# Preparing layer 1's row tiles during layer 0, and a start in another order

## The chip, the cores and the metric

The kernel runs on one core of a Trainium2 chip. The core has five engines that each work through a queue of their own, in order: TensorE for matmuls (PE in the profile, with its weight loads as PEld), VectorE (DVE), ScalarE (ACT), GpSimd (POOL) and SyncE (SP), which here only issues transfers. Transfers are carried out by 16 DMA engines that the queues share. The metric is the time of one execution on the device in microseconds (us); the time of a kernel is the median of several runs.

## The reference

The kernel computes two layers over 4096 rows of width 512. Each layer normalizes x, takes the positive part h, and adds a term to x.

Layer 0 is attention within 32 graphs of 128 consecutive rows, with a dense 4096 x 4096 matrix `adj` (mostly zeros) as a bias; outside a row's own graph the score is `-1e6` times twice the entry, and its softmax share is then masked to zero, yet counts in the denominator:

```python
h = jnp.maximum(_layernorm(x, axis=-1), 0.0)
query = h @ Wq.T + bq;  key = h @ Wk.T + bk;  value = h @ Wv.T + bv
a = jnp.where(mask, query @ key.T * scale, 0.0)
scores = (a + adj + adj) * jnp.where(mask, 1.0, -1000000.0)
x = x + (jax.nn.softmax(scores, axis=-1) * mask) @ value
```

Layer 1 is graph attention with 8 heads of 64 columns: each row averages the projected rows of its neighbours (`adj > 0`), weighted by `exp(t_j)` (the part of the logit that belongs to the row itself cancels in the softmax):

```python
h = jnp.maximum(_layernorm(x, axis=-1), 0.0)
mx = jnp.einsum('nf,hfd->hnd', h, W)
t_j = jnp.einsum('hnd,hd->hn', mx, a_dst)
attn = jax.nn.softmax(jnp.where(adj[None] > 0, s_i[:, :, None] + t_j[:, None, :], neg_inf), axis=-1)
x = x + concat_heads(jnp.einsum('hij,hjd->hid', attn, mx))
```

## The kernel before

Rows are worked on in 32 tiles of 128. The kernel has a start, layer 0, the rest of layer 1's preparation, and an aggregation.

**Start** (`fold`, line 163). The two weight matrices come in transposed. `fold` loads them, transposes them back on PE in blocks (line 185), and copies the blocks out of PSUM with ScalarE (line 186). It multiplies them into one matrix `m_sb` (line 221, four column blocks of four matmuls), so that a score needs one projection (`gT`, the "queries") and not two. Between the first transposes it spreads the two biases over all partitions by small matmuls against the identity (`spread_bias`, line 168), and VectorE multiplies these rows with the weights to get the bias columns `u_col` and `c_sb` (line 199). In the middle of the `m_sb` matmuls, PE spreads `u_col` into `u_sb` (line 211) and `zp` into `z_sb`.

**Layer 0** goes over 16 pairs of tiles (`for g in range(NG)`, line 525), pipelined: iteration g finishes pair g and starts pair g+1. Its pieces are
- `scores` (466): score matmuls, VectorE adds the diagonal block of `adj`, ScalarE takes the exponential;
- `queries` (408) of the next pair: 16 matmuls, each block copied out by ScalarE as `gT`;
- `turned` (485): the exponentials transposed by PE and copied to `sT` by ScalarE (487);
- for each of the two tiles: `read` (427) of a tile of the next pair, which takes two halves of 1 MB of `adj` that were loaded before, makes byte masks of them (VectorE, 136), sums the exponentials of all entries outside the graph (ScalarE, written to `junk`, 443), copies the diagonal block (GpSimd) and stores the masks to memory as `a_d`; `attend` (493), which multiplies `sT` with the values, adds x and stores the row tile to `x1_d`; `values` (420) of the next pair;
- `normed` (383) of pair g+2: statistics, normalization `hn`, transposes on PE (127), and the column sum `hu` (396).

Up to seven halves of `adj` are in flight (`AB = 7`): a new load is issued on SP when the oldest half has been read. Pairs of x rows (`xg`) have three buffers; SP issues them in the same queue as the halves. PSUM has four tiles named `pp` for queries, values, attention and projections together, and three named `pt` for transposes.

**Preparation of a layer-1 tile.** `normed1` (359) loads a row tile back from `x1_d` on SP, normalizes it and transposes it (127); `prepare` (367) projects it with `w1x` (`project1`, 243: eight matmuls into two `pp` tiles), ScalarE takes the exponential of `t_j`, VectorE multiplies the heads by it (`weigh`, 252), and ScalarE and GpSimd split the result into two parts of lower precision (`split`, 230 and 231). `w1x` is loaded in iteration 2. In the last iteration of layer 0, `prepare_on` is called four times: four row tiles are normalized and three of them are prepared. The loop at line 569 prepares the rest, 29 tiles.

**Aggregation** (line 590): for each of 32 row tiles, `aggregate` reads the masks back, turns them, and runs 96 matmuls over all prepared parts (283). VectorE and PSUM work for the first row tiles, and a check that the graphs are tiles (`graphs_are_tiles`, 298), already runs while the last tiles of layer 1 are prepared.

What sets the order: the program above gives dependences and buffers; a scheduler in the framework then fixes, when the kernel is built, an order of instructions for each engine by its own estimates of their durations. An engine follows that order strictly, and waits where an operand is not there yet. So an instruction can stand in another place of its queue than its line suggests, and a small edit moves others.

Of the kernel before, what the change touches and what calls it, by code (L numbers as in the profile page):

```python
# [51 lines left out]
def kernel(  # L52
# [110 lines left out]
    def fold(sb, tmp, work, ps_t, ps_p):  # L163
# [4 lines left out]
        def spread_bias(b):  # L168
            pp = ps_p.tile([P, D], F32, name="pp")
            for k in range(KC):  # L170
                nc.tensor.matmul(
                    pp[:, ts(k, P)], b[:, k : k + 1].to_broadcast([P, P]), ident,
                    start=True, stop=True,
                )
            row = work.tile([P, D], F32, name="b_row", tag="hn")
            nc.scalar.copy(row, pp)
            return row

        nat = []
        for n, wT in enumerate((wkT_sb, wqT_sb)):  # L180
            w = tmp.tile([P, KC, D], F32, name=f"w{n}", tag="lo")
            for k in range(KC):
                pt = ps_t.tile([P, KC, P], F32, name="pt")
                for m in range(KC):
                    nc.tensor.transpose(pt[:, m, :], wT[:, k, ts(m, P)], ident)
                nc.scalar.copy(w[:, :, ts(k, P)], pt)
                if n == 0 and k == 0:
                    rows = [spread_bias(b) for b in (bk_sb, bq_sb)]
# [6 lines left out]
        z_sb = sb.tile([P, 1], F32, name="z_sb")  # L195
        for dst, wT, row in ((u_col, wqT_sb, rows[0]), (c_sb, wkT_sb, rows[1])):
# [10 lines left out]
        for m in range(KC):  # L207
            if m == 2:
                pp = ps_p.tile([P, D], F32, name="pp")
                for k in range(KC):  # L210
                    nc.tensor.matmul(
                        pp[:, ts(k, P)], u_col[:, k : k + 1].to_broadcast([P, P]), ident,
                        start=True, stop=True,
                    )
                nc.scalar.copy(u_sb, pp)
                pp = ps_p.tile([P, D], F32, name="pp")
                nc.tensor.matmul(pp[:, :1], zp.to_broadcast([P, P]), one, start=True, stop=True)
                nc.scalar.copy(z_sb, pp[:, :1])
            pp = ps_p.tile([P, D], F32, name="pp")
            for k in range(KC):  # L220
                nc.tensor.matmul(
                    pp, wq[:, k, ts(m, P)], wk[:, k, :], start=(k == 0), stop=(k == KC - 1)
                )
            nc.scalar.mul(m_sb[:, m, :], pp, SCALE)
# [116 lines left out]
    with ExitStack() as straight:  # L341
# [4 lines left out]
        with ExitStack() as prep:  # L346
# [30 lines left out]
            with (  # L377
# [5 lines left out]
                def normed(g):  # L383
# [4 lines left out]
                    hns = []  # L388
# [520 lines left out]
```

## Time and profile before

| | us |
|---|---|
| median of 5 runs (lowest to highest) | 977.47 (976.46 to 978.88) |
| the profiled execution's own time | 976.75 |
| its span in the profile | 974.9 |
| PE busy / VectorE / ScalarE / GpSimd | 939.5 / 457.7 / 261.8 / 187.6 |
| first queries of layer 0 on PE | 37.57 |
| last scores of layer 0 on PE | 332.94 |
| aggregation on PE, from | 472.69 |
| aggregation matmuls on PE, busy | 489.6 |

Times in views of the trace count from the start of the span. A matmul on 32-bit operands leaves two records in the trace, so `x32` there is 16 matmuls. Where an engine was idle before an instruction, the trace names what ended the idle time. ScalarE and GpSimd are often idle, which costs nothing by itself; TensorE is idle for about 35 us of the span.

### The profile page before, as it was taken

How to read it: one execution, taken by the hardware profiler on the slowest of the kernel's cores; microseconds unless marked ns; L12 is line 12 of the kernel's file. 1: busy time of each engine (PE TensorE's matmuls, PEld its weight loads, DVE VectorE, ACT ScalarE, POOL GpSimd, SP SyncE). 2: the span in 40 equal slices, each digit the busy share in tenths (PEclk: the TensorE clock that was granted, in tenths of full speed). 3: DMA queues.
4: the chain of work that ended last, by engine and by line, in shares of the span. 5: the costliest groups of instructions: out<-in, count | busy, mean ns of one | idle time of the engine just before them, and what ended most of it. 6: DMA issues, size and time to landing. Idle time of an engine off the chain costs nothing.

```text
span 974.9 us, 13181 instructions
## 1 busy us (share of the span) xinstructions
PE 939.5 (96%) x5051; PEld 816.9 (84%) x5051; DVE 457.7 (47%) x978; ACT 261.8 (27%) x505; POOL 187.6 (19%) x344
## 2 busy tenths in 40 slices
PE   8999999999899979999999999999999999999994
PEld 5676676667666767888899999999999999999994
DVE  4677776667674387555142342423324233242321
ACT  5766666676651223333100000000000000000000
POOL 2221113112211065555110101101011010110100
PEclk9999999999999999999999999999999999999997
DMA  9988989999881232221022313123121221212201
GB/s 342 419 345 337 376 321 363 370 347 350 348 341 54 83 101 87 67 72 58 1 53 79 88 44 87 50 81 85 46 87 49 82 81 50 87 49 82 65 22 37
DMA packets 58042, 148.28 MB, mean 152 GB/s; under 512 B 6386, under 2 KB 23026, under 8 KB 49778
## 3 DMA queue, kind: packets, MB, share of 16 engines
q1 hardware_dynamic: 48178, 130.31, 38.0%
q10 hardware_dynamic: 9792, 17.05, 4.7%
q8 instruction: 41, 0.67, 0.3%
q14 instruction: 31, 0.25, 0.1%
HBM read 113.77 MB, written 33.55 MB: 151 GB/s over the span
## 4 chain that ended last, share of the span: by engine, by line
PE 79%; DMA 10%; DVE 4%; ACT 2%; POOL 1%; issue 1%; SPq 0%; ACTq 0%; DVEq 0%
PE pg L283 50%; PE pp L420 8%; DMA a<-adj 8%; PE pp L243 8%; PE pp L408 7%; PE pp L493 3%; PE pss L466 2%; PE pt L127 1%; ACT junk L443 1%; DMA bv_sb<-bv 1%; DVE row L121 1%; POOL part L231 1%; DVE a L136 1%; POOL rstd L120 1%; DVE stats L114 1%
## 5 line engine op out<-in xcount | busy, mean ns | idle before, releaser
L283 PE MATMUL pg<-part,at 128*128 128x348 f32 x3072 | 489.6, 321 | 1.2 <-DVE e L252 1.2
L283 PEld LDWEIGHTS pg<-part,at 128*128 128x128 f32 x3072 | 489.4, 188 | 1.5 <-issue 1.5
L277 DVE CAST at<-at 128x4096 fp32r<-128x4096 fp8e4 x32 | 73.6, 2300 | 312.2 <-PE pg L283 312.2
L290 ACT COPY tot<-pg 128x522 f32<-128x522 f32 x32 | 19.2, 599 | 470.5 <-PE pg L283 470.5
L443 ACT ACTIVATE junk<-a 128x2048 bf16<-128x2048 f32 (+15 forms) x92 | 124.5, 1353 | 47.6 <-DVE x L495 22.4
L243 PE MATMUL pp<-w1x,hT 128*128 128x256 f32 (+1 forms) x512 | 117.3, 383 | 0.0
L420 PE MATMUL pp<-wv,hT 128*128 128x512 f32 x256 | 114.9, 592 | 0.0
L408 PE MATMUL pp<-hT,m_sb 128*128 128x256 f32 x512 | 113.2, 379 | 0.0
L408 PEld LDWEIGHTS pp<-hT,m_sb 128*128 128x128 f32 x512 | 96.1, 190 | 12.9 <-issue 0.5
L243 PEld LDWEIGHTS pp<-w1x,hT 128*128 128x128 f32 x512 | 94.9, 190 | 13.8 <-issue 0.5
L420 PEld LDWEIGHTS pp<-wv,hT 128*128 128x128 f32 x256 | 48.6, 190 | 60.7 <-issue 60.7
L136 DVE TENSOR_SCALAR a<-a 128x512 fp8e4<-128x512 f32 x256 | 94.5, 450 | 2.0 <-DMA a_d<-a 2.0
L595 POOL COPY den_all<-tot 128x1 f32<-128x1 f32 x31 | 5.8, 186 | 369.1 <-DVE tot L291 369.1
L128 ACT ACTIVATE hT<-pt 128x512 f32<-128x512 f32 x64 | 37.3, 598 | 71.0 <-PE pt L127 71.0
L604 POOL TENSOR_TENSOR tot<-tot,row 128x512 f32<-128x512 f32 x31 | 40.0, 1290 | 61.7 <-DVE tot L296 61.7
L118 POOL TENSOR_SCALAR ve<-mv 128x1 f32<-128x1 f32 x64 | 17.2, 270 | 164.2 <-DVE mv L116 162.7
L231 POOL TENSOR_TENSOR part<-e,part 128x522 fp32r<-128x522 f32 x32 | 42.0, 1311 | 30.8 <-ACT part L230 27.2
L493 PE MATMUL pp<-v,sT 128*128 128x512 f32 x64 | 34.4, 618 | 8.5 <-ACT sT L487 8.0
L424 DVE TENSOR_TENSOR v<-pp,bv_sb 128x512 f32<-128x512 f32 x32 | 22.1, 690 | 42.0 <-PE pp L420 42.0
L270 DVE STREAM_TRANSPOSE at<-mw 128x1024 f32<-128x1024 f32 x32 | 39.6, 1236 | 0.0
L120 POOL TENSOR_TENSOR rstd<-ve,neghalf 128x1 f32<-128x1 f32 x64 | 38.5, 602 | 5.0
L252 DVE TENSOR_TENSOR e<-pp,e 128x256 f32<-128x256 f32 x64 | 26.5, 415 | 23.7 <-ACT e L371 21.0
(93 smaller groups left out, 586.3 us busy)
## 6 DMA issues: line engine op xcount, KB each, us to landing
a<-adj SPq DMA_DIRECT2D x64, 1024.0 KB, 12.5
a_d<-a SPq DMA_DIRECT2D x32, 512.0 KB, 10.8
row<-x_d SPq DMA_DIRECT2D x64, 256.0 KB, 3.2
mw<-a_d SPq DMA_DIRECT2D x128, 128.0 KB, 3.8
xg<-x SPq DMA_DIRECT2D x16, 512.0 KB, 4.5
x_d<-x ACTq DMA_DIRECT2D x32, 256.0 KB, 4.2
out<-tot ACTq DMA_DIRECT2D x31, 256.0 KB, 3.7
wkT_sb<-wkT SPq DMA_DIRECT2D x4, 256.0 KB, 4.9
```

Of the source, the lines that this page charges most:

```text
L120: nc.gpsimd.tensor_tensor(rstd, ve, neghalf, ALU.pow)
L136: nc.vector.tensor_scalar(a8v[:, u], av[:, u], 0.0, None, ALU.is_gt, saturate=False)
L231: nc.gpsimd.tensor_sub(dst[:, :, 1, :], e3, dst[:, :, 0, :].bitcast(F32))
L243: nc.tensor.matmul(pm[g][:, :n], hT[:, k, :], w1x[:, k, g * HW : g * HW + n], start=(k == 0), stop=(k == KC - 1),)
L270: nc.vector.transpose(at8.rearrange("p c n b -> p (c n b)").bitcast(F32).rearrange("p (c u n) -> p c u n", c=NW, n=B), mw.rearrange("p u ( ...
L277: nc.vector.tensor_copy(at.rearrange("p (c b) q -> p c b q", b=BY), at8.rearrange("p c q b -> p c b q"))
L283: nc.tensor.matmul(pg[:, c, : 2 * CW1], at[:, j, :], part(j)[:, c].rearrange("p s w -> p (s w)"), start=(j == 0), stop=(j == NT - 1),)
L408: nc.tensor.matmul(pp[:, : G * P], m_sb[:, k, ts(m, P)], hT[:, k, :], start=(k == 0), stop=(k == KC - 1),)
L420: nc.tensor.matmul(pp, hT[:, k, ts(t, P)], wv[:, k, :], start=(k == 0), stop=(k == KC - 1))
L443: nc.scalar.activation(junk[:, c0:c1], a[:, c0:c1], AF.Exp, scale=2.0 * NEG, accum_out=sums[:, n : n + 1],)
L493: nc.tensor.matmul(po, sT[:, t, :], v, start=True, stop=True)
L604: nc.gpsimd.tensor_add(num, num, row)
```

## The change

Two things change.

In `fold`, ScalarE and VectorE take turns in copying the transposed weights out of PSUM. The bias rows are spread only after all of `m_sb` has been multiplied, and `u_col` and `z` after the bias columns, in place of between the transposes and in the middle of the `m_sb` matmuls.

In layer 0, one layer-1 row tile is taken on in every second iteration from 3 on (3, 5, 7, 9, 11, 13), after `turned` and before the attention matmuls; each such step normalizes one tile and prepares the one before it. The last iteration has three such steps in place of four. So when layer 0 ends, nine tiles are normalized and eight prepared, in place of four and three; the loop after layer 0 prepares 24. `w1x` is loaded in iteration 1 in place of 2. In `normed`, the column sum `hu` of a tile comes right after its transposes. What is computed stays the same.

```diff
@@ fold
-        def spread_bias(b):
...
-                nc.scalar.copy(w[:, :, ts(k, P)], pt)
-                if n == 0 and k == 0:
-                    rows = [spread_bias(b) for b in (bk_sb, bq_sb)]
+                dst = w[:, :, ts(k, P)]
+                if k % 2:
+                    nc.vector.tensor_copy(dst, pt)
+                else:
+                    nc.scalar.copy(dst, pt)
...
+        for m in range(KC):
+            pp = ps_p.tile([P, D], F32, name="pp")
+            for k in range(KC):
+                nc.tensor.matmul(
+                    pp, wq[:, k, ts(m, P)], wk[:, k, :], start=(k == 0), stop=(k == KC - 1)
+                )
+            nc.scalar.mul(m_sb[:, m, :], pp, SCALE)
+        rows = []
+        for n, b in enumerate((bk_sb, bq_sb)):
+            pp = ps_p.tile([P, D], F32, name="pp")
+            for k in range(KC):
+                nc.tensor.matmul(
+                    pp[:, ts(k, P)], b[:, k : k + 1].to_broadcast([P, P]), ident,
+                    start=True, stop=True,
+                )
+            row = work.tile([P, D], F32, name=f"b_row{n}", tag="hn")
+            nc.scalar.copy(row, pp)
+            rows.append(row)
         for dst, wT, row in ((u_col, wqT_sb, rows[0]), (c_sb, wkT_sb, rows[1])):
...
-        for m in range(KC):
-            if m == 2:
-                pp = ps_p.tile([P, D], F32, name="pp")
-                for k in range(KC):
-                    nc.tensor.matmul(
-                        pp[:, ts(k, P)], u_col[:, k : k + 1].to_broadcast([P, P]), ident,
-                        start=True, stop=True,
-                    )
-                nc.scalar.copy(u_sb, pp)
...
-            nc.scalar.mul(m_sb[:, m, :], pp, SCALE)
+        pp = ps_p.tile([P, D], F32, name="pp")
+        for k in range(KC):
+            nc.tensor.matmul(
+                pp[:, ts(k, P)], u_col[:, k : k + 1].to_broadcast([P, P]), ident,
+                start=True, stop=True,
+            )
+        nc.scalar.copy(u_sb, pp)
+        pp = ps_p.tile([P, D], F32, name="pp")
+        nc.tensor.matmul(pp[:, :1], zp.to_broadcast([P, P]), one, start=True, stop=True)
+        nc.scalar.copy(z_sb, pp[:, :1])
@@ normed
-                    hns = []
                     for t in range(G):
                         hn = sb.tile([P, D], F32, name="hn")
                         norm(xg[g][:, t, :], hn)
                         relu_T(ps_t, hn, hT[:, :, ts(t, P)])
-                        hns.append(hn)
-                    for t, hn in enumerate(hns):
                         hu = sb.tile([P, D], BF16, name="hu", bufs=1)
@@ the loop of layer 0
-                    if g == 2:
+                    if g == 1:
                         w1x = load_w1(pool1, sb)
...
-                    def prepare_on():
-                        if last:
+                    def prepare_on(now):
+                        if now:
                             i = len(ahead)
                             ahead.append(normed1(i))
                             if i:
                                 prepare(i - 1, ahead[i - 1], part_tile(lo, i - 1))
 
                     s = scores(g, hT, gT, r, *look)
-                    prepare_on()
-                    prepare_on()
+                    prepare_on(last)
                     if not last:
                         ngT = queries(nhT)
                     sT = turned(s)
+                    prepare_on(3 <= g and g % 2)
                     nvs = []
                     for t in range(G):
                         look_on(t)
                         attend(sT, vs[t], g, t)
-                        prepare_on()
+                        prepare_on(last and t == 0)
                         if not last:
                             nvs.append(values(nhT, t))
```

## The prediction

> **What bounds the kernel now.** I read the page's shares first, then the chain that ended last in order of time, then the timeline of TensorE (PE) in three stretches: the start, layer 0, and the passage from layer 0 to layer 1.
>
> ```profile
> PE 939.5 (96%) x5051; PEld 816.9 (84%) x5051; DVE 457.7 (47%) x978; ACT 261.8 (27%) x505; POOL 187.6 (19%) x344
> ...
> PE   8999999999899979999999999999999999999994
> ...
> DMA  9988989999881232221022313123121221212201
> ...
> PE 79%; DMA 10%; DVE 4%; ACT 2%; POOL 1%; issue 1%; SPq 0%; ACTq 0%; DVEq 0%
> ```
>
> PE is busy in nearly every slice, in layer 0 too, where the DMA engines are also about 90% busy. So a change that only moves PE work can win no more than PE's idle time. Where that lies, PE's timeline shows. (Columns: start, length, instruction; in brackets the idle time before it and what ended it. One matmul leaves two records.) The start:
>
> ```profile
> 9.95 2.33 PE L185 MATMUL pt<-ident,wqT_sb 128*128 128x128 f32 x16
> 12.12 7.03 PE L221 MATMUL pp<-w,w 128*128 128x512 f32 x16
> 18.99 1.05 PE L211 MATMUL pp<-ident,u_col 128*128 128x128 f32 x8
> 19.88 0.28 PE L217 MATMUL pp<-one,zp 128*128 128x1 f32 x2
> 20.51 7.13 PE L221 MATMUL pp<-w,w 128*128 128x512 f32 x16 [0.35 <-ACT m_sb L224]
> 27.48 1.04 PE L127 MATMUL pt<-ident,hn 128*128 128x128 f32 x8
> 30.52 0.33 PE L127 MATMUL pt<-ident,hn 128*128 128x128 f32 x1 [2.00 <-DVE hn L121]
> 30.69 7.04 PE L420 MATMUL pp<-wv,hT 128*128 128x512 f32 x16
> 37.57 7.07 PE L408 MATMUL pp<-hT,m_sb 128*128 128x256 f32 x32
> ```
>
> From the bias sums to the first queries at 37.57 PE rests only 2.4 us: while it multiplies the weights, VectorE (DVE) finishes the bias columns and the first normalization. Layer 0:
>
> ```profile
> 54.92 1.13 PE L493 MATMUL pp<-v,sT 128*128 128x512 f32 x2 [0.61 <-ACT sT L487]
> ...
> 170.26 1.13 PE L493 MATMUL pp<-v,sT 128*128 128x512 f32 x2 [1.57 <-ACT sT L487]
> ...
> 189.31 1.12 PE L493 MATMUL pp<-v,sT 128*128 128x512 f32 x2 [0.74 <-ACT sT L487]
> ...
> 208.99 1.13 PE L493 MATMUL pp<-v,sT 128*128 128x512 f32 x2 [0.71 <-ACT sT L487]
> ...
> 249.23 1.13 PE L493 MATMUL pp<-v,sT 128*128 128x512 f32 x2 [2.90 <-ACT sT L487]
> ```
>
> With 0.61 at 111.57, 0.27 at 131.35 and 0.61 at 287.18, PE idles 8.0 us in 16 iterations, each time for sT. ScalarE (ACT) copies sT in its queue behind Exp pieces that wait for adjacency halves: in the chain the half asked for at 235.11 takes 11.35 us, and Exp, gT and sT follow before PE goes on at 249.23. The passage to layer 1:
>
> ```profile
> 351.52 0.66 PE L127 MATMUL pt<-ident,row 128*128 128x128 f32 x4 [2.23 <-DVE row L121]
> ...
> 365.36 0.66 PE L127 MATMUL pt<-ident,row 128*128 128x128 f32 x4 [3.28 <-DVE row L121]
> ...
> 388.93 0.60 PE L127 MATMUL pt<-ident,row 128*128 128x128 f32 x4
> 389.37 3.67 PE L243 MATMUL pp<-w1x,hT 128*128 128x264 f32 x16
> ```
>
> With 0.54, 0.78 and 0.50 more, 7.3 us of idle before the steady rhythm of 3.95 us a tile (transposes 0.44, projection 3.51).
>
> **Part by part. 1, the start.** I follow the built order of the changed kernel through its in-order queues with the durations above.
> - Alternate weight copies go to DVE, but between the first and second DVE copy the order has the statistics of the first x pair, whose load ends DVE's wait at 12.90 before. Two statistics (1.29), then the copy (no DVE row; ACT's takes 0.61, DVE's bias add from PSUM 0.69; I take 0.6): 14.8. Wq's last transposes (0.6) and a further DVE copy need it, so the weight products start near 15.7, not 12.12.
> - All sixteen now run in one piece, two groups of 6.9: to 29.6. The bias sums follow, 0.89 each (from 18.99 to 19.88): to 30.5 and 31.4. Before, they lay between the first transposes.
> - The bk row's copy (0.59) ends at 31.2. Only then can DVE make u_col. Its queue holds four column sums of u_col and one of c_sb (0.73 apart), two mask pieces (0.35) and then the first hn (0.54): 36.1.
> - PE transposes (0.45). ACT is in Exp pieces of 0.6, 1.8 and 2.1 with u_sb between, until about 37.5, so hT is there at 38.1 and PE does one values matmul. The next PE work is the transposes of tile 1's hn, which DVE reaches after three column sums, three masks and hu (4.4): 40.5. Transposed at 41.0; three matmuls of tile 0 (2.6) and four of tile 1 (3.4) end at 47.0.
>
> Queries thus start 47.0 - 37.57 = 9.4 us later; behind them wait every score and attention matmul, so it is on the path: +9.5. Ends: had the products started at 12.12 and nothing else moved, +6; +12 if PE runs cold. For that, the bk sums at 4.74 cost 1.9 us per 8 records, the same shape warm 1.05. Against it, after a gap of 3.28 us transposes took 0.66, after none 0.60, and my gaps are at most 1.8 us; no cold surcharge is taken. [...]
>
> **2, five projections and six row transposes inside layer 0.** Moved work is five times 3.51 and six times 0.44, 20.2 us of PE, out of the loop after layer 0 and into iterations 3 to 13; the last iteration keeps three projections. PE pays it in either place, and there the cover is only the 8.0 us of idle. Per moved tile the other queues get: SP one 256 KB row load (landing 3.2); DVE statistics, aggregate and norm (0.69, 0.17, 0.55) and two weighings (0.41 each); POOL two small steps (0.3, 0.6), the split (1.24) and a copy (0.19); ACT hT, Exp and cast (0.60, 0.18, 0.63). DVE, ACT and POOL are busy 33, 33 and 11 of 50 us in layer 0, so they fit; six row loads are 1.6 MB beside some 100 MB.
> - The projection lies between turned and attend in iterations 5, 7, 9, 11, 13, so sT has 3.5 us more there: the 0.74 of iteration 7 goes. The larger waits (1.57, 0.71, 2.90) fall in even iterations 6, 8, 10, which have no projection. They gain only by the extra 3.95 us that loads get in every second iteration; the three equal waits of 0.61 look like the floor, so at most 3.4 goes. SP does not use all of that time: its order puts the next x pair (which waits for both attends) ahead of adjacency loads, and it issued nothing from 238.4 to 255.46. I take -3.0 in all. Ends: -8.0 (all goes), and a loss, in the rivals.
> - Row loads sit on SP between adjacency loads, about one iteration ahead of the DVE statistics that wait for them; behind those wait masks and the values' bias add. A late row would cost up to 4.5 us, x's median landing time; issued 15 us ahead, nothing.
> - A split is 1.24 us alone and was 3.22 at 346.83 beside DVE's CAST; a diag copy 0.28 alone, 2.36 amid masks at 23.07. So five splits may take 3 us each in layer 0. POOL has 39 of 50 us free: nothing on the path. [...]
>
> **3, the passage.** PE waits there for row norms, and DVE carries two adjacency transposes and casts (1.24, 2.3 each) and the graph checks (sixteen steps of 0.42) among them. All of that stays, next to as many tiles. In the new order PE has one projection more ahead of the fifth row, but the sixth row now stands behind the second transpose and cast, which held the seventh before. I take -0.5; ends -7.3 and +3.
>
> **4, small edits.** w1x loads one iteration earlier (1.25 MB, landing 7.1, before adjacency loads on SP) and its eight DVE steps (0.68) move with it: 0, ends -1 and +1, since iterations 1 and 2 had no PE wait. hu right after each hn moves 0.68 us on DVE under 18 us iterations: 0. Aggregation, 489.6 us on PE, is untouched.
>
> **Sum.** +9.5 - 3.0 - 0.5 = +6.0 on the profiled execution's 976.75, thus 982.75. That execution was 0.72 below the median of 977.47, so for the median 983.5.
>
> **Rivals.** No change that can be told is within 0.2% (2.0 us), 975.5 to 979.4.
> - *Faster: the prepared tiles fill PE's waits.* Place: sT waits of layer 0 and norm waits of the passage. If the lead of prepared tiles removed all but 2.5 of 15.3 us, the sum is 9.5 - 12.8 = -3.3: 974. It decides once more than 9.5 + 2 is filled. For it: every wait has other PE work ready in principle. Against: PE runs in order, and the large waits are in iterations without a projection.
> - *Same: the late start is absorbed.* Loads run from the first microseconds whatever PE does, so a PE that starts 9.5 us later finds its adjacency there and the 8.0 go: +1.0, 978.5. Against: only seven halves fit, and the first wait of over 0.7 us came at 170, long after such a lead is spent.
> - *Much slower: a new wait on PSUM.* A projection takes two of four PSUM tiles that the second attend and values need 4.3 us later; the weighings that free them stand behind eight to fourteen masks (0.35 each, 2.8 to 4.9) and take 0.8, and masks wait for loads. It decides where masks and weighings outlast 4.3 us after the projection; at 2.5 us in five iterations, +12.5 on top: 995. For it: 3.6 to 5.7 stands against 4.3. Against: DVE idles a third of the time, so most of these masks can be done before the projection is.
>
> **How the numbers follow.** My forecast 0.58 (its own range 979.5 to 988), faster 0.13, same 0.13, much slower 0.16. Near the lower edge of the forecast a little falls to same. So faster 0.14, same 0.14, slower 0.72; the range 974 to 992 leaves out about half of the outer two.
>
> **What would show it.** Right: queries (line 406 then) start at 45 to 49, with idle before values; sT waits of at most 0.7 at most iterations; passage gaps of 5 to 8 us; aggregation starting 5 to 8 us later than 472.69. Wrong: queries before 43, waits of over 2 us before second attends, or passage gaps under 3 us.

## The result, and the profile after

The changed kernel takes 981.6 us (median of 50 runs, 977.48 to 984.8), the kernel before 978.5 us (median of 92 runs beside it). The ratio is 1.0030, with a 95% interval from 1.0022 to 1.0038: 2.9 us slower, where 6.0 us were forecast. The profiled execution took 980.02 us, with a span of 978.1, against 976.75 and 974.9 before: +3.2 us in the span.

The granted clock of PE differs too. Its mean is 0.992 over 68 recorded executions of the kernel before and 0.989 over 52 of the changed one, and within the kernel before the longer executions tend to be those with the lower clock (975.81 us at 0.995, 986.23 us at 0.986). By an estimate from these means, 0.003 of 978 us is 2.9 us of full clock more that was not granted; how much of it fell on work that the end waits for, these records do not tell.

The page of the changed kernel, in the same rows (busy time of each engine; busy tenths of PE in 40 slices; the clock granted to PE; the DMA engines; shares of the chain that ended last):

```profile
PE 943.3 (96%) x5051; PEld 817.6 (84%) x5051; DVE 461.2 (47%) x982; ACT 259.6 (27%) x501; POOL 187.1 (19%) x344
...
PE   6899999999999998899999999999999999999995
...
PEclk9899999999999999999999999999999999999998
DMA  9949999899983123322012222122231222312201
...
PE 86%; DMA 4%; DVE 3%; ACT 2%; POOL 2%; issue 1%; SPq 0%; ACTq 0%; DVEq 0%; POOLq 0%
```

PE is still the bound, and has as many instructions as before. What differs is at the left: the first slice of PE has 6 tenths in place of 8, and the second a granted clock of 8 tenths in place of 9. The third slice of the DMA row, 4 in place of 8, says that early in layer 0 the loads rest for a while: SP issued no adjacency load between 49.05 and 72.69 us. Before those loads its queue holds the load of a pair of x rows, which was issued at 71.03, as the second attention result of the first iteration was ready; in the kernel before that load went out at 61.27.

The windows view sums this up by stretch: from the start to the first queries, to the last scores of layer 0, to the first aggregation matmul, to the end. Its columns are the window, its length, then busy time and instructions of PE, PEld, DVE, ACT and POOL, the granted clock of PE, the DMA share and GB/s. After:

```profile
0.00:47.33 47.33, 35.73 (x114) 19.60 (x115) 26.96 (x74) 25.47 (x39) 7.53 (x27) 0.89 0.98 384
47.33:358.84 311.51, 307.76 (x1312) 215.40 (x1311) 205.19 (x545) 179.56 (x346) 71.47 (x129) 0.99 0.75 289
358.84:476.74 117.90, 110.54 (x555) 93.86 (x553) 75.19 (x167) 34.89 (x84) 61.10 (x125) 1.00 0.24 70
476.74:978.10 501.36, 489.27 (x3073) 488.79 (x3073) 153.86 (x196) 19.73 (x33) 46.96 (x63) 0.99 0.22 63
```

Before, these four stretches had lengths of 37.57, 295.37, 139.75 and 502.21 us. With the 20.2 us of moved PE work put back in its old place, the differences are:

| stretch | forecast | measured (profile) |
|---|---|---|
| start | +9.5 | 47.33 - 37.57 = +9.76 |
| layer 0 | -3.0 | 311.51 - 20.2 - 295.37 = -4.06 |
| passage | -0.5 | 117.90 + 20.2 - 139.75 = -1.65 |
| aggregation to the end | 0 | 501.36 - 502.21 = -0.85 |
| sum | +6.0 | +3.2 |

The start of the changed kernel on PE:

```profile
13.73 0.76 PE L174 MATMUL pt<-ident,wqT_sb 128*128 128x128 f32 x4 [3.21 <-DVE w L177]
14.29 15.53 PE L190 MATMUL pp<-w,w 128*128 128x512 f32 x32
...
36.11 1.09 PE L127 MATMUL pt<-ident,hn 128*128 128x128 f32 x4 [0.70 <-DVE hn L121]
38.47 2.08 PE L418 MATMUL pp<-wv,hT 128*128 128x512 f32 x2 [1.27 <-ACT hT L128]
40.34 1.06 PE L127 MATMUL pt<-ident,hn 128*128 128x128 f32 x4
41.19 6.30 PE L418 MATMUL pp<-wv,hT 128*128 128x512 f32 x14
47.33 1.03 PE L406 MATMUL pp<-hT,m_sb 128*128 128x256 f32 x4
```

The chain is the one foreseen: PE waits 3.21 us for a weight copy that stands behind the statistics of x on VectorE, then come the products, the late bias sums, and the first normalized tiles in two pieces. Two lengths are new. The products take 15.4 us, from 14.29 to the bias sums at 29.65, where before two halves of 6.9 us were enough; and the sixteen values records take 2.08 + 6.30 = 8.38 us, where before they took 7.04.

The waits for `sT` in layer 0, 8.0 us before, are now three, 3.3 us in all; around the first of them PE did this (the matmuls that the turned scores feed are in line 491 here, values in 418):

```profile
82.73 1.04 PE L127 MATMUL pt<-ident,hn 128*128 128x128 f32 x8
85.71 2.00 PE L491 MATMUL pp<-v,sT 128*128 128x512 f32 x2 [1.95 <-ACT sT L485]
87.51 4.46 PE L418 MATMUL pp<-wv,hT 128*128 128x512 f32 x8
91.81 1.02 PE L491 MATMUL pp<-v,sT 128*128 128x512 f32 x2
92.66 3.60 PE L418 MATMUL pp<-wv,hT 128*128 128x512 f32 x8
96.10 1.95 PE L464 MATMUL pss<-hT,gT 128*128 128x128 f32 x16
```

The same pair of instructions for the two tiles takes 91.81 - 85.71 = 6.10 us, and then 96.10 - 91.81 = 4.29. So the wait of 1.95 us cost 1.8 more in slow matmuls behind it. That is the clock, and it explains the long records of the start as well. Granted clock in small windows (the columns are window, length, PE busy, clock, DMA share, GB/s):

```profile
14.00:14.50 0.50, 0.50 (x5) 0.64 1.02 426
14.50:15.00 0.50, 0.50 (x1) 0.50 1.06 442
...
17.50:18.00 0.50, 0.50 (x2) 0.95 0.83 344
...
34.50:35.00 0.50, 0.39 (x2) 0.62 0.94 385
...
41.00:41.50 0.50, 0.50 (x3) 0.55 0.91 369
41.50:42.00 0.50, 0.50 (x2) 1.00 1.05 434
85.50:86.00 0.50, 0.29 (x1) 0.82 0.93 393
...
89.00:89.50 0.50, 0.50 (x2) 0.77 1.06 442
```

Next to the mixed windows the record reads 1.00 on one side and 0.50 on the other (1.00 from 14.00 to 14.10, 0.50 from 14.20 to 14.30), so a mean of 0.64 is read as 0.28 of the window at full clock and the rest at half. Read so, the clock is halved from 14.14 to 17.55, from 34.62 to 41.45, and from 85.82 to 89.23: for 3.4, 6.8 and 3.4 us.

In the passage the waits for normalized rows are 0.38, 3.02, 1.20 and 1.54 us, 6.1 in place of 7.3; the longest and the last of them:

```profile
388.00 0.66 PE L127 MATMUL pt<-ident,row 128*128 128x128 f32 x4 [3.02 <-DVE row L121]
...
404.76 0.66 PE L127 MATMUL pt<-ident,row 128*128 128x128 f32 x4 [1.54 <-DVE row L121]
```

### The profile page after: what moved, and what is told of

Same layout as the page of the kernel before. It is cut to its first block, busy times and chain, and to the rows that moved or that the text cites. A ratio compares the mean times of both kernels' runs of the same rounds, so it can differ in the third digit from the quotient of the medians.

```text
span 978.1 us, 13164 instructions
## 1 busy us (share of the span) xinstructions
PE 943.3 (96%) x5051; PEld 817.6 (84%) x5051; DVE 461.2 (47%) x982; ACT 259.6 (27%) x501; POOL 187.1 (19%) x344
## 4 chain that ended last, share of the span: by engine, by line
PE 86%; DMA 4%; DVE 3%; ACT 2%; POOL 2%; issue 1%; SPq 0%; ACTq 0%; DVEq 0%; POOLq 0%
PE pg L284 50%; PE pp L418 10%; PE pp L406 9%; PE pp L244 8%; DMA a<-adj 3%; PE pp L491 3%; PE pss L464 2%; PE pt L127 2%; PE pp L190 2%; ACT junk L441 1%; POOL part L232 1%; DMA xg<-x 1%; DVE a L136 0%; DVE row L121 0%; ACT gT L410 0%
## 5 line engine op out<-in xcount | busy, mean ns | idle before, releaser
L418 PE MATMUL pp<-wv,hT 128*128 128x512 f32 x256 | 117.1, 600 | 1.3 <-ACT hT L128 1.3
```

What stands on the lines that cost most here:

```text
L418: nc.tensor.matmul(pp, hT[:, k, ts(t, P)], wv[:, k, :], start=(k == 0), stop=(k == KC - 1))
```

## The experiments

My theory after the result: the change is two independent things, a start that loses time and moved preparations that gain less. The rival: the late start by itself takes waits out of layer 0, so that the parts don't add. Twelve kernels tell about this. In the table, "idle" is the stretch from the first queries to the last scores less PE's busy time in it, and "sT" is the part of the idle that ended with the copy of turned scores; both are of one profiled execution. The ratio is to the kernel before, run beside it on the same chip.

| kernel | median us | ratio (95%) | queries from | idle | sT | aggregation from |
|---|---|---|---|---|---|---|
| before | 978.5 | 1 | 37.57 | 8.5 | 8.0 | 472.69 |
| changed | 981.6 | 1.0030 (1.0022 to 1.0038) | 47.33 | 3.8 | 3.3 | 476.74 |
| moves + small edits | 972.2 | 0.9941 (0.9921 to 0.9961) | 39.07 | 5.2 | 2.4 | 469.83 |
| start alone | 984.9 | 1.0070 (1.0047 to 1.0094) | 48.26 | 4.4 | 3.8 | 478.81 |
| moves, even iterations | 972.5 | 0.9934 (0.9910 to 0.9958) | 39.03 | 4.6 | 2.2 | 469.44 |
| small edits alone | 978.4 | 1.0000 (0.9982 to 1.0018) | 37.31 | 8.5 | 8.1 | 474.95 |
| changed, copies by ScalarE | 976.4 | 0.9985 (0.9967 to 1.0003) | 45.65 | 3.7 | 3.4 | 474.39 |
| changed, bias sums early | 976.8 | 0.9992 (0.9976 to 1.0007) | 41.86 | 5.8 | 2.6 | 476.84 |
| before + 10.4 us of PE | 985.2 | 1.0073 (1.0045 to 1.0100) | 47.27 | 6.7 | 6.1 | 481.82 |
| changed + fillers | 979.0 | 1.0015 (0.9995 to 1.0034) | 48.17 | 3.2 | 2.8 | 475.42 |
| before + 3.5 us of PE | 978.2 | 0.9990 (0.9967 to 1.0014) | 39.79 | 8.4 | 8.0 | 474.11 |
| before + 20.8 us of PE | 999.0 | 1.0184 (1.0149 to 1.0220) | 54.87 | 11.4 | 11.0 | 494.08 |
| moves + small edits + 3.5 us | 973.5 | 0.9937 (0.9910 to 0.9963) | 40.12 | 2.7 | 2.4 | 467.56 |
| moves alone | 969.2 | 0.9886 (0.9853 to 0.9919) | 37.35 | 2.8 | 2.3 | 466.02 |

**Moves and small edits, with the old start.** `fold` is that of the kernel before.

```diff
@@ fold, against the changed kernel
...
-                dst = w[:, :, ts(k, P)]
-                if k % 2:
-                    nc.vector.tensor_copy(dst, pt)
-                else:
-                    nc.scalar.copy(dst, pt)
+                nc.scalar.copy(w[:, :, ts(k, P)], pt)
+                if n == 0 and k == 0:
+                    rows = [spread_bias(b) for b in (bk_sb, bq_sb)]
...
```

> The kernel before with the new layer 0 (preparation in iterations 3 to 13, w1x loaded in iteration 1, hu after each hn) and the old start. Theory A, two independent parts: the queries start near 37.6 again, the shorter idle of layer 0 and of the passage stays, 5 to 7 us faster than before, ratio 0.993 to 0.995. Rival B, the late start is what let the adjacency loads get ahead and so emptied the waits of layer 0: most of the gain goes, at most 2 us faster, ratio 0.998 to 1.001, with sT waits of 6 us or more in layer 0.

Measured: 0.9941, that is 5.8 us under the kernel before. Of sT waits, 8.0 us before, 2.4 are left. One new wait came, for a row that VectorE had not normalized in time:

```profile
218.56 0.44 PE L127 MATMUL pt<-ident,row 128*128 128x128 f32 x2 [2.46 <-DVE row L121]
```

So the moves are worth more than the 3.5 us forecast for layer 0 and the passage together.

**The new start alone.** The loops are those of the kernel before.

```diff
@@ the loop of layer 0, against the changed kernel
...
-                    if g == 1:
+                    if g == 2:
                         w1x = load_w1(pool1, sb)
...
-                    prepare_on(3 <= g and g % 2)
...
```

> The kernel before with the new start alone. Theory A: queries start near 47.3, and nothing gives the 9.8 us back: ratio 1.008 to 1.011. Rival B: PE starts later but finds its adjacency halves ready, layer 0's 8.0 us of waits shrink to 3 or 4: ratio 1.004 to 1.006, with last scores only 5 to 6 us later than 332.94.

Measured: 1.0070, +6.8 us, between the two expectations, for a start that is 10.7 us late. The rest did not come from preparations, for none was moved. The profile shows where it went: layer 0 has four sT waits in place of eight.

```profile
159.96 1.13 PE L494 MATMUL pp<-v,sT 128*128 128x512 f32 x2 [0.27 <-ACT sT L488]
198.72 1.13 PE L494 MATMUL pp<-v,sT 128*128 128x512 f32 x2 [1.43 <-ACT sT L488]
237.73 1.12 PE L494 MATMUL pp<-v,sT 128*128 128x512 f32 x2 [1.67 <-ACT sT L488]
275.46 1.13 PE L494 MATMUL pp<-v,sT 128*128 128x512 f32 x2 [0.40 <-ACT sT L488]
```

The waits, 3.8 us in sum, are those that the rival expected. The late start is partly absorbed, then. The forecast's argument against it (seven buffers are soon used up) did not hold.

**The preparations in even iterations.** The prediction gave a reason by parity: sT is covered only in iterations that hold a projection.

```diff
@@ the loop of layer 0, against moves + small edits
-                    prepare_on(3 <= g and g % 2)
+                    prepare_on(4 <= g and g % 2 == 0)
```

> As the first of these runs, but with the preparation in iterations 4, 6, 8, 10, 12 and 14, where the kernel before had its larger waits for sT (1.57, 0.71, 2.90 in iterations 6, 8, 10). If the projection helps by lying between turned and attend, this variant hides these waits directly: 1 to 2 us faster than the odd one. If it helps by giving the loads more time in every second iteration, the two are within 1 us of each other.

Measured: 0.9934 against 0.9941, and the sT waits 2.2 against 2.4 us. So the time does not depend on which iterations hold the projections, and the waits of iterations 6, 8 and 10 are gone with either choice: a projection beside the wait is not needed to take it away. A wait for a row of 1.97 us came here too, at 236.63.

**The small edits alone** (the earlier `w1x`, and `hu` after each `hn`).

```diff
@@ against the kernel before
-                        hns.append(hn)
-                    for t, hn in enumerate(hns):
...
-                    if g == 2:
+                    if g == 1:
                         w1x = load_w1(pool1, sb)
```

> The kernel before with only the two small edits: w1x loaded in iteration 1, hu right after each hn. Theory A: no difference that can be told, ratio 0.999 to 1.001. Rival C, the small edits reorder the queues of layer 0 and are themselves a part of its gain: ratio 0.995 to 0.998.

Measured: 1.0000, with the same sT waits in sum as before (8.1 us). They are worth nothing alone, as forecast. One more thing is in this profile: the wait at iteration 10, the longest of the kernel before, here has slow matmuls behind it, which it had not there.

```profile
249.16 2.07 PE L490 MATMUL pp<-v,sT 128*128 128x512 f32 x2 [2.92 <-ACT sT L484]
...
260.89 1.95 PE L463 MATMUL pss<-hT,gT 128*128 128x128 f32 x16
```

Before, that matmul took 1.13 us after a wait of 2.90, and the next scores came 257.91 - 249.23 = 8.68 us after its start, not 260.89 - 249.16 = 11.73. The granted clock from 250 to 254 is 0.50 here and was 1.00 there. The same wait can cost its own length, or that and a stretch at half clock, which cost 3.1 us here.

**All weight copies by ScalarE.**

```diff
@@ fold, against the changed kernel
                 dst = w[:, :, ts(k, P)]
-                if k % 2:
-                    nc.vector.tensor_copy(dst, pt)
-                else:
-                    nc.scalar.copy(dst, pt)
+                nc.scalar.copy(dst, pt)
```

> The changed kernel, but ScalarE alone copies the transposed weights, so that no weight copy stands behind the statistics of x on VectorE. In the changed kernel the last four transposes waited 3.21 us for such a copy, the products began at 14.29 instead of 12.12 and took 15.4 us instead of 13.9, at a granted clock of 0.77 to 0.81 in their first slices. Theory A (the copy costs both its wait and a cold clock behind it): the products begin at 11.5 to 12.2 and take 13.9, the queries begin at 43 to 44 instead of 47.33. Rival (no clock surcharge from the wait): the products begin there, take 15.4 still, and the queries begin at about 45. For the whole: if the start were simply added to the rest, the time falls by 3.5 to 4 us against the changed kernel, to 977.5 to 978; if the waits of layer 0 share in it (they shrink when the start is later), by 1.5 to 2.5, to 979 to 980. The order built for ScalarE and TensorE in layer 0 is that of the changed kernel.

Measured: 0.9985, that is 1.0030 - 0.9985 = 0.45% or 4.4 us under the changed kernel.

```profile
12.99 14.22 PE L187 MATMUL pp<-w,w 128*128 128x512 f32 x32
...
33.51 0.63 PE L127 MATMUL pt<-ident,hn 128*128 128x128 f32 x4 [1.01 <-DVE hn L121]
35.57 2.08 PE L415 MATMUL pp<-wv,hT 128*128 128x512 f32 x2 [1.43 <-ACT hT L128]
37.44 1.11 PE L127 MATMUL pt<-ident,hn 128*128 128x128 f32 x4
38.34 7.48 PE L415 MATMUL pp<-wv,hT 128*128 128x512 f32 x14
```

The wait for the copy is gone and the products take 14.1 us again: the bias sums begin at 27.05 in place of 29.65, 2.6 us earlier. But the queries begin only 1.7 us earlier, at 45.65 and not at 43 to 44, since the values took 2.08 + 7.48 = 9.56 us in place of 8.38: the clock was halved from 34.12 to 40.95 (0.56 granted from 34 to 35, 0.50 from 35 to 40, 0.52 from 40 to 41), as long as in the changed kernel, and more of the values fell into it. Layer 0 takes 309.78 us in place of 311.51, with no slow matmuls behind a wait in it in this profile (a granted clock of 1.00). The two profiled executions are only 2.8 us apart in all; the 4.4 us by the ratios is more than either expectation, and the profiles do not account for the rest.

**The bias sums back between the first transposes** (the alternating copies stay).

```diff
@@ fold, against the changed kernel
+        def spread_bias(b):
...
+                if n == 0 and k == 0:
+                    rows = [spread_bias(b) for b in (bk_sb, bq_sb)]
             nat.append(w)
...
-        rows = []
-        for n, b in enumerate((bk_sb, bq_sb)):
...
```

> The changed kernel, but with the sums of the two bias rows back between the first transposes, so that the chain after the products (sums, copies of the rows, the products with the weights on VectorE, the sum of u, first halves of x) is not late. Theory A (the late bias sums are the larger part of the 9.8 us at the start): the queries begin at 40 to 42 instead of 47.33. In the built order the halves read ahead of the turned scores are those of the kernel with the early fold (10.6 before the first, 14.5 before the second), not those of the changed kernel (11.6 and 15.5). If the parts add, the time falls by 5 to 7 us to 975 to 977; if the pool of waits in layer 0 is shared between the late start and the preparations, half of it comes back as waits: 978 to 979, with 2 us more of waiting for the turned scores than the changed kernel's 3.3.

Measured: 0.9992, 3.7 us under the changed kernel, and queries at 41.86, 5.5 us earlier.

```profile
15.28 2.82 PE L185 MATMUL pt<-ident,wqT_sb 128*128 128x128 f32 x12 [4.12 <-DVE w L188]
17.90 14.80 PE L203 MATMUL pp<-w,w 128*128 128x512 f32 x32
...
33.57 1.07 PE L127 MATMUL pt<-ident,hn 128*128 128x128 f32 x8
```

The queries begin as early as expected, although the wait for the copy on VectorE grew to 4.12 us: with the bias columns done early, PE goes from the products to the values without a pause of over 0.25 us. So the late bias sums are the larger part of the late start, and the copy the smaller. Of the 5.5 us about two thirds are in the time, which lies where the expectation without shared waits put it. The waits for sT that the other expectation asked for did not come back (2.6 us); a wait of 2.88 us for a row did, at 221.89. The profiled execution, 980.25 us, was the slowest of its twelve, so its later stretches are not read here.

**The kernel before, with 10.4 us more PE work in its start.** Three of the four products of the weights are made twice.

```diff
@@ fold, against the kernel before
-        for m in range(KC):
+        for m in (0, 1, 3, 0, 1, 2, 3):
             if m == 2:
```

> The kernel before with nothing but more work for TensorE in the start: three of the four products of the weights are made twice (24 more matmuls of the kind that take 13.9 us for 32, so 10.4 us), at a warm clock. Nothing of the new order of the start is in it. Theory (a late TensorE by itself empties the waits for the turned scores, 8.0 us before): the queries begin at 48, the turned scores are waited for 3 to 4.5 us, layer 0 is 3 to 4.5 us shorter, the aggregation starts 6 to 7 us later, and the time is 984 to 986. Rival (the waits went because of the new order of the start, its small edits or chance): the waits stay at 7 to 9 us and the time is 988 to 990. The built order has 13.6 halves read before the first turned scores, 3 more than before, so this run does not tell whether the shorter waits come from the time or from the order that it leads to.

Measured: 1.0073, +7.1 us, with an interval from +4.4 to +9.8. The time fits the theory, but the profile doesn't: queries 9.7 us late, sT waits of 6.1 us in sum, layer 0 as long as before (295.25 us at a granted clock of 0.99; behind its longest wait, of 2.53 us, the pair of instructions took 6.10 us, and the next pair 4.29), and the aggregation 9.1 us late. A late start doesn't by itself empty the waits as it did in the kernel with the new start alone.

**Fillers for PE between 31 and 41 us.**

```diff
@@ against the changed kernel
+                pt = ps_t.tile([P, KC, P], F32, name="pt")
+                for k in range(n):
+                    nc.tensor.transpose(pt[:, k % KC, :], ident, ident)
...
```

Four of them stand behind the bias sums, four behind `z_sb`, eight behind the first transposes of x.

> The changed kernel with 16 transposes of the identity more, read by nobody, that fill TensorE's pauses between 31 and 41 us, where the granted clock stood at 0.83 and 0.50 with pauses of no more than 1.3 us. Theory (a sparsely used TensorE is granted less, and this is paid at the first halves of x and values): the granted clock is 0.95 or more from 32 to 44, the first two products of the values take 1.1 to 1.3 us instead of 2.08, and the queries begin at 46 to 47.3, in spite of up to 1 us of transposes that the pauses do not hold. Rival (the granted clock there is that of another cause): it stays below 0.85 in the slices from 36 to 40, and the queries begin at 48 or later. The time of the whole within 1.5 us of the changed kernel either way.

Measured: 1.0015, with an interval that overlaps that of the changed kernel; no verdict on the time. In the profile the two values records after the pause took 1.10 us in place of 2.08 and all of the values 7.27 in place of 8.38:

```profile
40.37 1.10 PE L429 MATMUL pp<-wv,hT 128*128 128x512 f32 x2
```

But the queries began at 48.17, since the start was later already at the products (15.31 in place of 14.29) and the fillers stand ahead of the values. The granted clock was 1.00 up to 37, 0.55 from 37 to 38, 0.50 from 38 to 40 and 0.74 from 40 to 41: the slow stretch is 3.4 us long in place of 6.8, and was not prevented, so the theory's 0.95 up to 44 did not come. The mean granted clock of the twelve executions is 0.993, against 0.989 for the changed kernel, which fits a part of its slow stretches being filled away. One thing stays open: the products took 16.1 us here, with records of up to 1061 ns at a granted clock that reads 1.00, so the record of the clock may not be complete.

**3.5 us more PE work: the order of the late start, without the lateness.** The scheduler then builds ScalarE's queue in layer 0 with the same count of halves read before each of the 16 copies of turned scores as in the kernel with the new start alone.

```diff
@@ fold, against the kernel before
-        for m in range(KC):
+        for m in (0, 0, 1, 2, 3):
             if m == 2:
```

> The kernel before, with one of the four products of the weights made twice: 8 matmuls or 3.5 us more for TensorE in the start, and nothing else. That is enough to change the order built for layer 0: before each of the 16 copies of turned scores ScalarE has as many halves read (11.6, 15.5, 19.4, 23.2, 27.1, 32.0 and so on) as in the kernel with the new start alone, which begins its queries 10.7 us later than the kernel before and idled 4.4 us on TensorE in layer 0 instead of 8.5. Theory 1 (the order built for layer 0 sets its waits): TensorE's idle time from the first queries to the last scores is 4 to 5 us as there, layer 0 is 4 us shorter, and the time is within 1.5 us of the kernel before in spite of 3.5 us more work. Theory 2 (it is the later start on the chip, by which more halves lie ready): a third of the lateness takes a third of the effect; idle 7 us or more, and the time 2 to 3.5 us over the kernel before.

Measured: 0.9990, queries at 39.79, and these waits for sT:

```profile
97.41 1.13 PE L493 MATMUL pp<-v,sT 128*128 128x512 f32 x2 [2.29 <-ACT sT L487]
...
192.35 1.13 PE L493 MATMUL pp<-v,sT 128*128 128x512 f32 x2 [1.31 <-ACT sT L487]
...
231.51 1.13 PE L493 MATMUL pp<-v,sT 128*128 128x512 f32 x2 [1.82 <-ACT sT L487]
...
289.07 1.13 PE L493 MATMUL pp<-v,sT 128*128 128x512 f32 x2 [1.17 <-ACT sT L487]
```

With 0.27, 0.27 and 0.86 they make 8.0 us, and layer 0 takes 295.37 us, to the hundredth as before. Theory 1 falls: the order is that of the kernel with 3.8 us of waits, and the waits are those of the kernel before. Theory 2 has the idle time right (8.4 us) and not the time, which by the ratio is 3.2 us under to 1.4 us over the kernel before. Between this kernel and the one with the new start alone, the large difference is the time at which PE enters layer 0: 39.79 here, 48.26 there.

**20.8 us more PE work.**

```diff
@@ fold, against the kernel before
-        for m in range(KC):
+        for m in (0, 1, 3, 0, 1, 3, 0, 1, 2, 3):
             if m == 2:
```

> The kernel before, with six products of the weights more, 48 matmuls or 20.8 us for TensorE in the start; 15.5 halves are read ahead of the first turned scores. The queries begin at 58. Theory 1 (the waits are those of the built order, a late start as such is paid in full): idle of TensorE in layer 0 of 4 to 7 us, and the time 17 to 21 us over the kernel before. Theory 2 (a later start by itself empties the waits): with 5 halves more in hand nothing is waited for, idle below 3 us, and the time 14 to 16 us over it.

Measured: 1.0184, +18 us for a start that is 17.3 us late, with 11.0 us of sT waits, more than before and more than either theory had. Theory 2 falls as well: this late start is paid in full. A new theory fits all the kernels without moved work: what empties waits is a start that is later than the built order counts on. Where PE's extra work is in the program, the order reads as many halves more ahead of each copy of turned scores (13.6 and 15.5 before the first, in place of 10.6), and uses up the lead; the waits are 8.0, 6.1 and 11.0 us. In the new start PE enters layer 0 8.5 us later than in the run with the same counts, and the waits are 3.8; by the theory the halves lie ready by then. This is not shown: it was formed after the runs, and only the pair with the same counts of halves bears on it. About 20 of ScalarE's some 380 instructions up to the last copy of turned scores stand in other places between those two, and the copies and bias work of the start differ as well.

**Moves and small edits with 3.5 us more PE work.**

```diff
@@ fold, against moves + small edits
-        for m in range(KC):
+        for m in (0, 0, 1, 2, 3):
             if m == 2:
```

> The kernel with the moved preparations and the early fold (queries at 39.07, idle of TensorE in layer 0 of 5.2 us, 5.8 us under the kernel before), with one product of the weights more (3.5 us), so that the order built for layer 0 becomes nearly that of the changed kernel (11.6 halves before the first turned scores, 23.2 before the fourth, 36.8 before the seventh). Theory (order and moves draw on the same waits): queries at 42.5, idle 3.5 to 4.5 us, the time 3 to 5 us under the kernel before, that is 1 to 3 us over the kernel with the moves alone and 6 to 8 us under the changed kernel, whose start is 4.8 us later still. Rival (the extra work is simply added): 2 us under the kernel before.

Measured: 0.9937, 6.2 us under the kernel before, so not worse than without the extra work. The new wait for the row at 218.56 is gone, and layer 0 has 2.7 us of idle. The queries begin 2.8 us later than with the moves alone (the last kernel below). That is better than both expectations. In the profiles the sT waits are the same (2.4 us in both) and the wait for the row makes the difference in idle time; the times by the ratio, 0.9937 and 0.9941, cannot be told apart.

**The moves alone,** with the old start and both small edits undone.

```diff
@@ against moves + small edits
+                        hns.append(hn)
+                    for t, hn in enumerate(hns):
...
-                    if g == 1:
+                    if g == 2:
                         w1x = load_w1(pool1, sb)
```

> The moved preparations alone: early fold, and the two small edits undone as well (the products of halves of x with u after both halves, the weights of layer 1 loaded in the third iteration). Without the moves the small edits measured 1.000 of the kernel before. Theory (the moves carry the gain): 4.5 to 7 us under the kernel before, queries at 37.5, TensorE idle in layer 0 for 4.5 to 6 us. Rival (the moves gain only in company with the small edits, by the earlier weights): 3 us under it or less, with new waits at the first projections.

Measured: 0.9886 (0.9853 to 0.9919), 969.2 us: the fastest of all, 11.2 us under the kernel before by the ratio, 9.5 by the medians. It beats both kernels: the changed one has a span 10.6 us longer. The windows of its three later stretches, with the columns as above:

```profile
37.35:345.87 308.52, 305.75 (x1312) 214.59 (x1310) 207.54 (x552) 181.37 (x350) 62.12 (x131) 1.00 0.79 306
345.87:466.02 120.15, 113.39 (x554) 96.09 (x553) 75.21 (x167) 34.77 (x84) 61.17 (x125) 0.97 0.23 68
466.02:967.50 501.48, 489.89 (x3073) 489.41 (x3073) 153.82 (x196) 19.77 (x33) 46.98 (x63) 0.99 0.22 63
```

Against the kernel before, the start gives -0.2, layer 0 308.52 - 20.2 - 295.37 = -7.1, the passage +0.6, the rest -0.7: -7.4 us in the span. That is less than the 11.2 us of the ratio, and these two executions are not the typical ones: that of the kernel before was granted a clock of 0.995, where the 20 beside this kernel have 0.991 in the mean, and this one 0.991, where its six have 0.994. No wait for sT is left after 173 us, that is, after the first moved preparations. The rival falls: the moves need no small edits. Two things set this kernel apart from the one with moves and small edits (971.0 us of span): that one's wait of 2.46 us for a row, with 5.99 us behind it for a pair of instructions that next took 4.29, isn't here, and in that one's start the values took 8.74 us after a wait of 2.00, where here they took 7.04 after a wait of 2.01. In the kernel with moves and small edits:

```profile
30.33 0.33 PE L127 MATMUL pt<-ident,hn 128*128 128x128 f32 x1 [2.00 <-DVE hn L121]
30.50 8.74 PE L417 MATMUL pp<-wv,hT 128*128 128x512 f32 x16
```

The second is a stretch at half clock (a granted clock of 0.91 from 30 to 50 us there, 1.00 up to 37.35 here) that the same wait does not bring in every execution. Whether the first belongs to the small edits stays open, as the kernel with 3.5 us more PE work has them and not the wait.

## Why the prediction was right, and where it was not

The forecast was slower by 6.0 us, and it is slower by 2.9; the direction, the range and the main mechanism held. The sum hides some steps that failed.

- **Start, +9.5: measured +9.76.** The chain was read rightly: the copy behind the statistics of x, the bias sums after the products, PE waiting for `hn` in two pieces, queries at 47.33 where 47.0 was worked out. But that the size is right is luck, since errors cancel. The first pair of x was there at 11.80 and not at 12.90, so the products began at 14.3 and not at 15.7 (-1.4). And "no cold surcharge is taken" was wrong: the clock was halved twice in the start, which cost 15.36 - 13.9 = 1.5 us in the products, so that the bias sums began at 29.65 where 29.6 was worked out, and 8.38 - 7.04 = 1.3 us in the values. Not all of the second is in the late queries, as the second tile's `hn` was there at 39.9 and not at 40.5. The argument against a surcharge was a wait of 3.28 us in the passage that had cost nothing. One such row proves little: over the passage the granted clock was 1.00 in 4 of the 14 profiled executions and 0.97 to 0.99 in the other 10; and the wait at 249 was free in one execution and had 3.1 us behind it in another.
- **Layer 0, -3.0: measured -4.06,** of which PE's idle is -4.7 and slower matmuls +0.7. The step took the moves to be the only thing that shortens waits. In the profiles the moves alone are worth -7.1 there (idle 8.5 to 2.8), and the new start alone also takes out 4.0 us of idle. Together they took 4.7, which fits both drawing on the same 8.0 us. So the gain of the moves was put too low, and in the changed kernel it doesn't add to the late start's. Of the reasons given, the extra time for loads fits the runs (with the moves alone no sT wait is left after 173 us, in even iterations as in odd) but was not tested by itself; the cover by a projection in the same iteration is not needed; and 0.61 us was no floor: with the moves alone two of the three equal waits stay, both ahead of the first moved projection, and the third, at 287, went.
- **Passage, -0.5: measured -1.65.** The waits fell from 7.3 to 6.1 us, within the 5 to 8 that was to show the step right; the other 0.4 us is PE's busy time.
- **The aggregation was left at zero and was 0.85 us shorter.** Nothing in it was changed, and over all the kernels it took 500.9 to 502.6 us, so this is what two profiled executions differ by.
- **Rivals.** The wait on PSUM did not come: no wait of over 0.25 us between 50 and 370 us is on an attention matmul or values for anything but sT. "The late start is absorbed" was given 0.13 and is true in part: with the new start alone 10.7 us become 6.8. The argument against it, that a lead is spent long before the first large wait, fails: in that kernel the first wait of over 0.7 us came at 198.72 and not at 170.26. Why the lead lasts so long is not shown. "The prepared tiles fill PE's waits" is true in part of the moves without the new start: of 15.3 us of waits 7.9 were left, 2.3 for sT and 5.6 for rows, where 2.5 were thought possible, and the time was 11.2 us lower (7.9 to 14.4).
- **Signs.** The queries came at 45 to 49, and the waits were as said. The aggregation did not begin 5 to 8 us later than 472.69 but 4.05, at 476.74, by the gains that had been put too low.

What made the change slow is therefore the start: against the moves alone, the changed kernel's aggregation begins 10.7 us later, 9.98 of them already at the first queries. Its parts are settled in the order of size only: bias sums made late (5.5 us at the queries when put back), copies on VectorE (1.7 us there), with half-clock stretches in both.

## What to carry to other kernels

When a change moves work into idle time and also delays the bound engine, the two may be paid from the same waits: list the waits, and count each once. Lateness of the bound engine can be partly free: 10.7 us cost 6.8 with the new start alone, while 17.3 us cost 18 when the same engine was simply given more work. That it turns on whether the order fixed at build time counts on the lateness is a theory here, resting on one pair of runs. And before work on the bound engine's start is put in another order, look at what each late small step releases on the other engines: here 1.8 us of bias sums, moved behind 13.9 us of products, were the larger part of a late start of 9.8 us.

## What the runs showed of the hardware

In these runs a pause of PE had a price besides its length. In the changed kernel waits of 1.95 and of 3.21 us were each followed by 3.4 us at half clock; a wait of 2.0 us in the old start was followed by values in 7.04 us in one execution and 8.74 in another. So one such stretch costs 1.5 to 1.8 us. Behind the wait at 249 in the kernel with the small edits alone, where the granted clock was 0.62 from 248 to 250 and 0.50 from 250 to 254, the extra time was 3.1. For waits of 2.0 to 3.3 us such a stretch comes in some executions and not in others: after 3.28 us the transposes took 0.66 in the kernel before and 1.11 in the one with the new start alone.

Which it is, the traces tell in part. In the changed kernel the clock was halved at 14.14, 34.62 and 85.82, and the distances, 20.48 and 51.20 us, are 6 and 15 times 3.413, where its two shorter slow stretches are 3.41 long: in this execution the stretches begin on one grid. In the 3.41 us ahead of each, PE was busy for 0.41, 1.98 and 1.46 us, a share of 0.12, 0.58 and 0.43. The wait of 3.02 us at 388.00, which cost nothing more, is divided by the grid: PE was busy for 2.20 us of one step and 1.61 of the next, 0.64 and 0.47, and the granted clock stayed at 1.00. The share alone does not separate them, as 0.58 stands ahead of a halving and 0.47 does not. That a wait costs more when it lies mostly inside one step of the grid is my estimate from these few stretches, and is not shown.

The longest slow stretch of the changed kernel had no long pause before it: from 31 to 38 us PE was busy between 0.2 and 0.9 of each microsecond, with no single wait over 1.3 us, and the clock was halved from 34.62 to 41.45.
